# A hand-planned attention block: another account of VectorE's time, other due times, and queries, gating and normalization given out at other places

## The chip, the cores and the metric

The kernel runs on one core of a Trainium2 chip. The metric is the time of one execution on the device in microseconds (us). The kernel before was timed in three runs: 564.36, 565.13 and 567.15, a median of 565.13.

## The reference

The input x has 2 batches of 1024 tokens of 512 channels, all in fp32. Each token is normalized; the result feeds a causal attention with 32 heads of 16 channels, and a gate: a linear layer plus the sum of two of eight low-rank experts (rank 16), chosen for each token. The output is x + s * g.

```python
xn = _layernorm(x)                                   # over the 512 channels
# attention: h = 32 heads, hd = 16
q, k, v = (heads(xn @ W.T + b) for W, b in ((Wq, bq), (Wk, bk), (Wv, bv)))
scores = einsum('bhqd,bhkd->bhqk', q, k) / sqrt(hd)
att = softmax(where(causal, scores, -inf))
s = einsum('bhqk,bhkd->bhqd', att, v).reshape(b, l, d) @ Wo.T + bo
# gate: E = 8 experts of rank R = 16, TOP_K = 2, SCALING = 1
base = xn @ W_base.T + b_base
top_p, top_i = top_k(softmax(xn @ W_gate.T), 2)      # top_p divided by its sum
route_w = sum(one_hot(top_i, E) * top_p[..., None])
delta = einsum('bner,eor->bno', einsum('bnd,erd->bner', xn, A) * route_w[..., None], B)
g = silu(base + delta * SCALING)
out = x + s * g
```

## The kernel before

**Engines and queues.** TensorE (PE) does the products, ScalarE (ACT) the exponentials of the softmax and some copies, VectorE (DVE) evictions, sums and the normalization, GpSimd (POOL) the causal masks, and SyncE (SP) issues nearly all DMAs. Each engine executes its instructions in the order in which the program gives them out. That order is not left to a scheduler: the program is written by a planner in Python that runs once, when the kernel is built.

**The plan.** The attention is cut into units (b, oc, c): a batch, a group of eight heads (128 channels), and a half of 512 queries. A unit with c = 0 has 5 steps, one with c = 1 has 13; a step is a set of key tiles against queries. There are 144 steps. For step n the program gives out, in this order:

- `scores(n)` (from L1513): first what stands in the list `urgent` and is due (placing of keys and queries by DMA), then the score products s <- qT, kT (L1529), then two exponentials pt <- s on ScalarE (L1540);
- the masks of the step on GpSimd (`masked`, L1557: pt <- pt);
- `values(n - 1)` (L1562): the value products av <- pt, v (L1581) with the pt of the step before; at the end of a unit av is copied to oT and avs;
- `fill(n)` (L1426): other work, in small portions, so that TensorE is occupied while ScalarE makes the exponentials.

**Filler work.** `Task` objects are Python generators with a due step, a cost in TensorE's time and conditions. In `fill`, tasks that have a cost give out products until a share is used up; the share is the rest of all work over the rest of the steps, and from step 12 (L1448) it is raised where the work due by some step needs it. After the products, work without a cost on TensorE is given out in this order: entries of `splits`, of `later` (functions with the step from which they may run), tasks without a cost (L1493), then weight blocks (`issue_parts`, L1503), then one or two entries of `late`, which hold evictions of finished product groups.

**The account.** All DVE and ACT instructions go through `Metered` (L40, its call is L56, so L56 is the line of all of them in the profile). It adds up when the engine will be free: 0.09 us plus elements over a rate (930 per us for DVE, 1020 for ACT). `late_by` (L1410) compares DVE's account with the time at which the next step's evictions begin, and `enough(more)` (L1478) says whether `more` us of work would be too late. An entry of `patient` is kept for another step at its first turn if `enough()` is true, and a task without a cost is stopped if its due step is still ahead and `enough(2.0)` (`layernorm_task`) or `enough(0.65)` (others) holds. `SV` = 1.9 stands for the time of scores and values in a step.

**Products by blocks.** The big products (queries and keys "q", values, gate and output "p") are made from 2 x 2 blocks with seven products in place of eight. That needs sums of weight blocks (`four_sums` in `combine_task` and `qk_weights_task`; made once, in place, then stored to DRAM as "kept" and loaded again when needed) and sums of token blocks ("asum", `sums_task`, on DVE). `matmul` (L228) gives out each of the products, 128 x 128 against 256 or 512 columns, as four instructions; it is the line of all filler products. Evictions add the seven products up in kf, qf, v, g and x. Names: ph is the product for routing and experts, pq, pk and pv those of the first unit, made directly.

- `issue_parts` (L613) loads weight blocks ("w" from an input, "wt" from kept, 256 KB each) in the fixed order of their use, up to NWP = 4 ahead of the oldest in use. SP waits at such a load until the buffer's last reader is done.
- `qk_weights_task(n)` (L631) prepares the query and key weights of head group n: for n = 0 to 3 it loads them raw (two DMAs of 256 KB, L123), puts them in pairs with an ACT copy, makes four sums in place on DVE, waits a step, stores them (kept, 1 MB, L640), waits twice more and sets `qk_ready[n]`. For n from 4 (second batch) it loads what was kept. The weights have two buffers. The next load's task waits for `len(qk_ready) >= n` and for the end of the products with the weights of n - 2.
- `split` (L485) turns the finished queries and keys of a unit into qT and kT: DVE and ACT operations, in `later`, then a copy on ACT (`remainder`), then two placing DMAs (L483) put in `urgent` for the next step.
- `layernorm_task(b, c)` (L264): loads x, `statistics` (DVE; then the power -1/2 on GpSimd, L250), subtraction and scaling (DVE), then transposes (sq <- x, DVE), a store to DRAM (scr, L301) and four loads (xnT, L308), in two halves of two channel groups. There is one buffer for sq. For b = 0 the whole second chunk's layernorm falls in the first steps of attention.
- `out_task` (L874): `final` is called with the eviction of an output block; it multiplies by half the gate, adds x, and queues the store, and the load of the next block's x and gate.
- `post` (L1007) normalizes a unit's outputs by the denominators, which go out to DRAM (den, L1020), come back spread (dens, L1025), are inverted, go out (back, L1028) and come back (avs, L1045), whence DVE's rb.

The program ends with a guard that reads a flag and would run a second, general version if scores were out of bounds; here it doesn't run.

Of the kernel before, what the change touches and what calls it, by code (L numbers as in the profile page):

```python
# [13 lines left out]
ALU = mybir.AluOpType  # L14
# [12 lines left out]
KC = D // P  # L27
# [12 lines left out]
class Metered:  # L40


    def __init__(self, engine, rate=930):
        self.engine, self.ready, self.free, self.rate = engine, 0.0, 0.0, rate

    def __getattr__(self, name):
        def run(*args, **named):
            sizes = [1]
            for a in (*args, *named.values()):
                if hasattr(a, "shape"):  # L50
                    n = 1
                    for k in a.shape[1:]:
                        n *= k
                    sizes.append(n)
            self.free = max(self.free, self.ready) + 0.09 + max(sizes) / self.rate
            return getattr(self.engine, name)(*args, **named)  # L56

        return run
# [23 lines left out]
def direct(ctx, tc, sound, x, wq, wk, wv, wo, wb, wa, wg, wB, bq, bk, bv, bo, bb, out):  # L82
# [7 lines left out]


    nc = tc.nc
    ve = Metered(nc.vector)
    act = Metered(nc.scalar, 1020)
    NB, L, _ = x.shape
    C = 512
    NC = L // C
# [119 lines left out]
    WAIT = object()  # L217
    PAUSE = object()
    turned_at, now = {}, [0]
# [44 lines left out]
    def layernorm_task(b, c):  # L264


        xt = chunk_tile(b, c)
        for i in range(NS):
            i0 = c * C + i * P
            nc.sync.dma_start(  # L270
                out=xt[i * SQ : (i + 1) * SQ],
                in_=x[b, i0 : i0 + P].rearrange("(t r) d -> r t d", r=SQ),
            )
        if b == 0:
            load_rest()
        tiles = [xt[:, t] for t in range(TT)]
        for _ in range(3 if b else 1):
            yield WAIT
        s = yield from statistics(tiles, b > 0)
        if b:  # L280
            yield WAIT
        for t in range(0, TT, 2):
            normalize(tiles[t : t + 2], s[0][:, t : t + 2], s[1][:, t : t + 2])
            yield PAUSE
        if b:
            yield WAIT
        xnT = sb.tile([P, KC, C], F32, tag="xnT", bufs=3, name=f"xnT_{b}_{c}")
        for k0 in range(0, KC, 2):
            sq = sb.tile([P, 2, NS, TT, SQ], F32, tag="sq", bufs=1, name="sq")
            for t in range(TT):  # L290
                yield PAUSE
                ve.transpose(
                    out=sq[:, :, :, t],
                    in_=tiles[t][:, k0 * P : (k0 + 2) * P].rearrange(
                        "p (k q d) -> p k q d", k=2, q=NS
                    ),
                )
            scr = dram.tile([NS, SQ, 2, NS, TT * SQ], F32, tag="scr", name="scr")

            def store(sq=sq, scr=scr):  # L300
                nc.sync.dma_start(  # L301
                    out=scr.rearrange("i d k q m -> (i d) (k q m)"),
                    in_=sq.rearrange("p k q t r -> p (k q t r)"),
                )

            def place(k0=k0, scr=scr):
                for q in range(NS):
                    nc.sync.dma_start(  # L308
                        out=xnT[q * SQ : (q + 1) * SQ, k0 : k0 + 2].rearrange(
                            "d k (i m) -> d k i m", i=NS  # L310
                        ),
                        in_=scr[:, :, :, q].rearrange("i d k m -> d k i m"),
                    )

            if not b:
                store()
                place()
                continue
            later.append((now[0] + b, store))
            later.append((now[0] + b + 1, place))  # L320
            for _ in range(0 if k0 else 1 + b):
                yield WAIT
        xnTs[b, c] = xnT
        turned_at[b, c] = now[0] + b
# [160 lines left out]
    def split(b, oc, c, qf, kf):  # L485

        qT, kT = split_tiles(b, oc, c)
        split_keys(kT, kf, kf)

        def queries():  # L490
            split_queries(qT, qf)
            room["acc"] += 1
            later.append((now[0] + 1, remainder))

        def remainder():
            copy_remainder(qT)
            urgent.append((now[0] + 1, lambda: place_queries(qT)))

        by = starts[b, oc, c]
        costs[queries], costs[remainder] = (1.1, by - 4), (0.6, by - 3)  # L500
        later.append((now[0] + 1, queries))
        urgent.append((now[0] + 1, lambda: place_keys(kT, kf)))
# [117 lines left out]
    def qk_weights_task(n):  # L620

        oc = n % KC
        if n >= KC:
            wqks.append(sb.tile([P, 4 * KC, P], F32, tag="wqk", bufs=2, name=f"wqk{oc}"))
            nc.sync.dma_start(out=wqks[n], in_=qk_kept[oc])
        else:
            if n >= 2:
                wqks.append(load_qk(oc))
                for _ in range(3):
                    yield WAIT  # L630
                pair_up(wqks[n])  # L631
                yield WAIT
            w = wqks[n]
            yield from four_sums(
                {(i, j): w[:, 4 * j + 2 * i : 4 * j + 2 * i + 2] for i in range(2) for j in range(2)},
                {t: w[:, 2 * KC + 2 * t - 2 : 2 * KC + 2 * t] for t in range(1, 5)},
            )
            qk_kept[oc] = dram.tile([P, 4 * KC, P], F32, tag=f"kept_qk{oc}", bufs=1, name="kept")
            yield WAIT
            nc.sync.dma_start(out=qk_kept[oc], in_=w)  # L640
            for _ in range(2):
                yield WAIT
        qk_ready[n] = now[0] + (2 if n >= KC else 0)
        yield WAIT

    def tokens(k):
# [227 lines left out]
    def out_task(k):  # L874

        _, b, c = stages[k]
        y, g = block_of(chunk_tile(b, c)), block_of(g_tiles[b, c])
        order = [(0, 0), (1, 1), (0, 1), (1, 0)]
        xts, gts = {}, {}

        def block(t, i, j):
            rows = slice(c * C + BK * i, c * C + BK * i + BK)
            return t[b, rows, BK * j : BK * j + BK].rearrange("(t p) o -> p t o", p=P)

        def load():
            i, j = order[len(xts)]
            xts[i, j] = sb.tile([P, 2, BK], F32, tag="xr", name=f"xr_{b}_{c}_{i}{j}")
            nc.sync.dma_start(out=xts[i, j], in_=block(x, i, j))
            gts[i, j] = sb.tile([P, 2, BK], F32, tag="gr", name=f"gr_{b}_{c}_{i}{j}")
            nc.sync.dma_start(out=gts[i, j], in_=g(i, j))  # L890

        def final(i, j):
            ve.scalar_tensor_tensor(y(i, j), y(i, j), 0.5, gts[i, j], ALU.mult, ALU.mult)
            ve.tensor_tensor(y(i, j), y(i, j), xts[i, j], ALU.add)

            def store():
                nc.sync.dma_start(out=block(out, i, j), in_=y(i, j))

            later.append((now[0] + 2, store))
            if i == j:  # L900
                later.append((now[0] + 2 - i, load))

        load()
        load()
        yield from block_task(k, y, final)
# [395 lines left out]
    for b in range(NB):  # L1301
        for c in range(NC):
# [24 lines left out]
            if not b and not c:  # L1327
# [13 lines left out]
                    )  # L1341
                for n in range(2 * KC):
                    Task(
                        (20, 13, 26, 32)[n] if n < KC else -9, qk_weights_task(n), 0.0, after=9,
                        ready=lambda n=n: n < 2 or (
                            now[0] > qk_done.get(((n - 2) // KC, (n - 2) % KC, 1), now[0])
                            and len(qk_ready) >= n
# [23 lines left out]
                )  # L1371
            else:
                before = starts[b, KC - 1, c] + 2
                Task(len(plan) - 9, bases_task(b, c), 0.0, after=before - 12, takes={"xnT": 2})
                n = len(units) - 3
                Task(len(plan) - 12, test_task(0, n, 0), 0.0, after=before - 10)
                Task(
# [26 lines left out]
    last_work = 13 * MM  # L1404
    spent = 0.0
    late, active = [], []
    SV = 1.9
    clock = [15.0]

    def late_by(n, begins, more):  # L1410
# [4 lines left out]
            return free - begins  # L1415
        if plan[n - 1][3] and plan[n - 1][0] != units[-1]:
            free = max(free, begins + 2.0) + 1.3
        return free - (begins + SV + 1.7 + 0.7)

    def turn_late():  # L1420
        late.sort(key=lambda x: x[0])
# [4 lines left out]
    def fill(n):  # L1426
# [18 lines left out]
        elif n < begin:  # L1445
            even = min(even, (total - last_work - spent) / (begin - n))
        share = spent + even
        if n >= 12:  # L1448

            left = 0.0  # L1450
            for x in tasks:
# [41 lines left out]
        for x in [x for x in tasks if not x.cost]:  # L1493
# [1 line left out]
                continue  # L1495
            said = PAUSE
            while said is not None and said is not WAIT:
                if x.due > n and enough(2.0 if x.steps.__name__ == "layernorm_task" else 0.65):
                    break
                said = x.step()  # L1500
            x.waiting = said is WAIT
        clock[0] = begins
        issue_parts()  # L1503
        for _ in range(1 if active or len(plan) - 5 < n < len(plan) else 2):
            if late and (min(x[0] for x in late) <= n or not within):
# [4 lines left out]
        for par, kt, q0, _, _ in plan[n][1]:  # L1510
            last_pieces.setdefault((par, q0 == C - P), []).append((n, kt, q0))

    def scores(n):  # L1513
        (b, oc, c), pieces, _, _ = plan[n]
        for x in [x for x in urgent if x[0] <= n]:
            urgent.remove(x)
            x[1]()
        ss = [ps_s.tile([P, 2, C], F32, tag="s", name=f"s{p}") for p in range(2)]
        for m, (par, kt, q0, w, col) in enumerate(pieces):
            first_unit = (b, oc, c) == units[0]  # L1520
# [581 lines left out]
```

## Time and profile before

One execution was profiled. It took 567.24 us; its span on the core, first to last instruction, is 565.51.

| what | value |
|---|---|
| median of the three timed runs | 565.13 us |
| the profiled execution, whole | 567.24 us |
| its span | 565.51 us |
| granted TensorE clock, mean | 0.992 of full |
| instructions | 19451 |
| ACT: exponentials pt <- s | 288, 1024 ns each |
| POOL: masks pt <- pt | 224, 512 ns each on average |
| DMA | 79.16 MB, 140 GB/s on average |

How to read the views that follow. The page gives each engine's busy time, its share of the span and the number of instructions; below it the span in 40 equal slices of 14.1 us, a digit being the busy share in tenths (9 is 90% or more), and "PEclk" the granted clock in tenths. In the list of waits, a line names the engine, operation and line that waited, then what released it, then the sum in us, the number of waits and the longest. A line of the timeline has the start, the time until the end, the engine, its line, the operation, written and read tiles, shape, and xcount for the number of like instructions put together; in brackets the engine's idle time just before and what ended it. "SPq" lines are the moments at which SP's queue issued a DMA, not the transfer itself. Busy times are near the limit here: what is left is where TensorE stands still.

### The profile page before, as it was taken

What the parts mean: (1) busy time and instruction counts of PE and PEld (TensorE: products, weight loads), DVE (VectorE), ACT (ScalarE), POOL (GpSimd) and SP (SyncE); (2) the same over time, 40 slices, a digit from 0 to 9 for tenths busy, and PEclk for the clock granted to TensorE, in tenths of its full rate; (3) what the DMA queues carried; (4) which work ended last, traced back from release to release, by engine and by line L of the source; (5) the groups of instructions that cost most, each with busy time, mean ns of one, the idle gap of its engine ahead of it and who ended that gap; (6) DMA issues with size and microseconds to landing.
All of it is one profiled execution on the core that took longest, in us unless ns stands there. A gap on an engine that the chain in (4) does not pass through costs nothing.

```text
span 565.5 us, 19451 instructions
## 1 busy us (share of the span) xinstructions
PE 543.5 (96%) x8411; PEld 283.0 (50%) x8411; DVE 334.5 (59%) x693; ACT 351.8 (62%) x389; POOL 119.0 (21%) x248
## 2 busy tenths in 40 slices
PE   8999998899999999999998999999999999999994
PEld 8434554454445554544644554444545554456551
DVE  4444556557477675566569546684257644649833
ACT  2427852576777766757656765747667777776540
POOL 2213400110114430230213330220103330120400
PEclk9999998999999999999999999999999999999997
DMA  8632576154723663651564633660124223552211
GB/s 254 175 131 78 188 261 208 64 190 134 207 77 139 224 227 118 184 157 60 171 188 152 212 126 114 220 187 23 42 72 157 80 79 90 181 167 82 96 39 45
DMA packets 65198, 79.16 MB, mean 140 GB/s; under 512 B 9560, under 2 KB 52576, under 8 KB 63696
## 3 DMA queue, kind: packets, MB, share of 16 engines
q1 hardware_dynamic: 65088, 77.83, 42.7%
q8 instruction: 68, 1.11, 0.8%
q14 instruction: 26, 0.21, 0.1%
q10 hardware_dynamic: 16, 0.00, 0.0%
HBM read 46.39 MB, written 19.37 MB: 116 GB/s over the span
## 4 chain that ended last, share of the span: by engine, by line
PE 84%; DVE 9%; DMA 2%; ACT 2%; issue 1%; POOL 0%; SPq 0%; DVEq 0%; POOLq 0%; ACTq 0%
PE av L1581 23%; PE p L228 21%; PE s L1529 16%; PE q L228 13%; DVE x L56 3%; PE po L228 2%; PE ph L228 2%; PE pv L228 1%; PE pq L228 1%; PE pk L228 1%; ACT pt L56 1%; PE warm L183 1%; DMA qT<-qT 1%; DVE oT L56 1%; PE pq_first L350 1%
## 5 line engine op out<-in xcount | busy, mean ns | idle before, releaser
L56 ACT ACTIVATE pt<-s 128x1024 f32<-128x1024 f32 x288 | 290.5, 1024 | 166.8 <-PE s L1529 155.7
L1557 POOL TENSOR_SCALAR_AFFINE_SELECT pt<-pt 128x256 f32<-128x256 f32 (+1 forms) x224 | 111.0, 512 | 413.9 <-ACT pt L56 413.0
L1581 PE MATMUL av<-pt,v 128*32 128x512 f32 (+3 forms) x1680 | 158.8, 467 | 3.0 <-DVE oT L56 1.9
L1529 PE MATMUL s<-qT,kT 32*128 32x512 f32 (+3 forms) x1616 | 108.9, 365 | 1.8 <-DMA qT<-qT 1.1
L1529 PEld LDWEIGHTS s<-qT,kT 32*128 32x128 f32 x1616 | 62.4, 184 | 61.2 <-issue 34.4
L1581 PEld LDWEIGHTS av<-pt,v 128*32 128x32 f32 x1680 | 42.6, 109 | 58.5 <-issue 39.7
L228 PE MATMUL p<-wt,asum 128*32 128x256 f32 x960 | 59.8, 383 | 2.2 <-DVE m L56 2.2
L228 PE MATMUL q<-asum,wqk 128*32 128x256 f32 x832 | 51.2, 379 | 3.2 <-DVE kf L56 3.2
L228 PEld LDWEIGHTS p<-wt,asum 128*32 128x32 f32 x960 | 31.8, 111 | 31.1 <-issue 12.1
L228 PEld LDWEIGHTS q<-asum,wqk 128*32 128x32 f32 x832 | 26.5, 110 | 27.9 <-DVE kf L56 6.9
L228 PE MATMUL q<-xnT,wqk 128*32 128x256 f32 x624 | 39.6, 379 | 0.0
L56 DVE TENSOR_TENSOR g<-p,g 128x512 f32<-128x512 f32 x20 | 13.8, 690 | 28.1 <-PE p L228 28.1
L56 DVE SCALAR_TENSOR_TENSOR kf<-q,kf 128x256 f32<-128x256 f32 x39 | 16.5, 422 | 23.5 <-PE q L228 23.1
L228 PEld LDWEIGHTS q<-xnT,wqk 128*32 128x32 f32 x624 | 20.0, 110 | 19.0 <-issue 6.0
L228 PE MATMUL p<-w,xnT 128*32 128x256 f32 x448 | 28.1, 379 | 0.0
L228 PEld LDWEIGHTS p<-w,xnT 128*32 128x32 f32 x448 | 15.8, 110 | 10.6 <-issue 4.2
L228 PE MATMUL p<-w,asum 128*32 128x256 f32 x320 | 20.6, 379 | 0.0
L56 DVE TENSOR_TENSOR v<-p,v 128x512 f32<-128x512 f32 x15 | 10.3, 687 | 12.8 <-PE p L228 12.7
L228 PEld LDWEIGHTS ph<-wag_sb,xnT 128*32 128x32 f32 x512 | 15.4, 110 | 3.8 <-issue 2.7
L228 PE MATMUL ph<-wag_sb,xnT 128*32 128x136 f32 x512 | 16.9, 279 | 0.0
L228 PE MATMUL po<-wo,oT 128*32 128x512 f32 x128 | 16.5, 593 | 0.4 <-ACT oT L56 0.4
L56 DVE TENSOR_TENSOR qT<-qf,qT 128x512 fp32r<-128x512 f32 x15 | 10.3, 686 | 9.9 <-ACT qT L56 9.9
(145 smaller groups left out, 561.4 us busy)
## 6 DMA issues: line engine op xcount, KB each, us to landing
wt<-kept SPq DMA_DIRECT2D x40, 256.0 KB
qT<-qT SPq DMA_DIRECT2D x30, 256.0 KB
x<-in_x_dram SPq DMA_DIRECT2D x16, 256.0 KB
kept<-wqk SPq DMA_DIRECT2D x4, 1024.0 KB
wqk<-kept SPq DMA_DIRECT2D x4, 1024.0 KB
kT<-kf SPq DMA_DIRECT2D x30, 128.0 KB
scr<-sq SPq DMA_DIRECT2D x6, 512.0 KB
xnT<-scr SPq DMA_DIRECT2D x24, 128.0 KB
```

The source lines that it names most:

```text
L56: return getattr(self.engine, name)(*args, **named)
L183: nc.tensor.matmul(warm[:, n % 4 * P : n % 4 * P + P], lhsT=ident, rhs=ident, start=True, stop=True)
L228: nc.tensor.matmul(o[j : j + 32], lhsT=lhsT[:, j : j + 32] if len(lhsT.shape) == 2 else lhsT[:, j // 32], rhs=rhs, start=start, stop=stop,)
L350: nc.tensor.matmul(ps[:, cols], lhsT=w[:, k, :], rhs=xnT[:, k, cols], start=k == 0, stop=k == KC - 1)
L1529: nc.tensor.matmul(ss[s // 2][:, s % 2, col : col + w], lhsT=keys[rows, kt % TT * P : kt % TT * P + P], rhs=q[rows, halves * par + half_, ...
L1557: nc.gpsimd.affine_select(out=d, in_=d, compare_op=ALU.is_ge, fill=0.0, base=0, pattern=[[0, d.shape[1]], [1, P]], channel_multiplier=-1,)
L1581: nc.tensor.matmul(avs_now[par][32 * s : 32 * s + 32, q0 : q0 + w], lhsT=vs[b, kt][:, h * VS - HD * par : h * VS - HD * par + HP], rhs=pt[ ...
```

## The change

Both versions give out the same number of instructions. The change alters when.

1. The account: DVE 0.19 us plus elements / 966 (before 0.09, 930), ACT 0.22 plus elements / 1274 (before 0.09, 1020). `SV` is 1.7 (1.9). A task without a cost stops at `enough(1.85)` if its due step is over 20 steps ahead, else at 0.65; the special value for layernorm goes.
2. Layernorm: the first batch's chunks too wait a step between DVE's statistics and GpSimd's power, and there is a wait for the next step after each half's store and loads.
3. Queries: their placing becomes due in the same step, and `fill` gives out what is urgent just ahead of the weight blocks.
4. Query and key weights: `qk_ready[n]` is set before the step's wait that stands ahead of the store, so up to three steps earlier; the tasks n = 2, 3 are due at 24 and 28 (26, 32).
5. Output blocks: the two gating operations, the store and the next load become one function, in `later` and `patient`, so that evictions can go ahead of it.
6. The rule that raises a step's share for due work holds from step 5 (12). `bases_task` is due 7 steps before the end (9).

```diff
-    def __init__(self, engine, rate=930):
+    def __init__(self, engine, base, rate):
...
-            self.free = max(self.free, self.ready) + 0.09 + max(sizes) / self.rate
+            self.free = max(self.free, self.ready) + self.base + max(sizes) / self.rate
...
-    ve = Metered(nc.vector)
-    act = Metered(nc.scalar, 1020)
+    ve = Metered(nc.vector, 0.19, 966)
+    act = Metered(nc.scalar, 0.22, 1274)
...
-        s = yield from statistics(tiles, b > 0)
+        s = yield from statistics(tiles, True)
...
                 store()
                 place()
+                yield WAIT
                 continue
...
-            urgent.append((now[0] + 1, lambda: place_queries(qT)))
+            urgent.append((now[0], lambda: place_queries(qT)))
...
+            qk_ready[n] = now[0]
             yield WAIT
             nc.sync.dma_start(out=qk_kept[oc], in_=w)
             for _ in range(2):
                 yield WAIT
-        qk_ready[n] = now[0] + (2 if n >= KC else 0)
+        qk_ready.setdefault(n, now[0] + 2)
         yield WAIT
...
         def final(i, j):
-            ve.scalar_tensor_tensor(y(i, j), y(i, j), 0.5, gts[i, j], ALU.mult, ALU.mult)
-            ve.tensor_tensor(y(i, j), y(i, j), xts[i, j], ALU.add)
+            def gated():
+                ve.scalar_tensor_tensor(y(i, j), y(i, j), 0.5, gts[i, j], ALU.mult, ALU.mult)
+                ve.tensor_tensor(y(i, j), y(i, j), xts[i, j], ALU.add)
+                later.append((now[0] + 2, store))
+                if i == j:
+                    later.append((now[0] + 2 - i, load))
...
-            later.append((now[0] + 2, store))
-            if i == j:
-                later.append((now[0] + 2 - i, load))
+            patient.append(gated)
+            later.append((now[0], gated))
...
-                        (20, 13, 26, 32)[n] if n < KC else -9, qk_weights_task(n), 0.0, after=9,
+                        (20, 13, 24, 28)[n] if n < KC else -9, qk_weights_task(n), 0.0, after=9,
...
-                Task(len(plan) - 9, bases_task(b, c), 0.0, after=before - 12, takes={"xnT": 2})
+                Task(len(plan) - 7, bases_task(b, c), 0.0, after=before - 12, takes={"xnT": 2})
...
-    SV = 1.9
+    SV = 1.7
...
-        return free - (begins + SV + 1.7 + 0.7)
+        return free - (begins + SV + 2.4)
...
-        if n >= 12:
+        if n >= 5:
...
-                if x.due > n and enough(2.0 if x.steps.__name__ == "layernorm_task" else 0.65):
+                if x.due > n and enough(1.85 if x.due > n + 20 else 0.65):
...
         clock[0] = begins
+        place_urgent(n)
         issue_parts()
...
+    def place_urgent(n):
         for x in [x for x in urgent if x[0] <= n]:
             urgent.remove(x)
             x[1]()
+
+    def scores(n):
+        (b, oc, c), pieces, _, _ = plan[n]
+        place_urgent(n)
```

More of the change, by code (lines that the diff above doesn't have):

```diff
@@ L40 @@
 class Metered:
-    def __init__(self, engine, rate=930):
-        self.engine, self.ready, self.free, self.rate = engine, 0.0, 0.0, rate
+    def __init__(self, engine, base, rate):
+        self.engine, self.ready, self.free, self.base, self.rate = engine, 0.0, 0.0, base, rate
     def __getattr__(self, name):
@@ L1511, in direct @@
             last_pieces.setdefault((par, q0 == C - P), []).append((n, kt, q0))
-    def scores(n):
-        (b, oc, c), pieces, _, _ = plan[n]
+    def place_urgent(n):
         for x in [x for x in urgent if x[0] <= n]:
```

## The prediction

> **What bounds the kernel now.** First the page: shares of each engine and the 40 slices.
>
> ```profile
> PE 543.5 (96%) x8411; PEld 283.0 (50%) x8411; DVE 334.5 (59%) x693; ACT 351.8 (62%) x389; POOL 119.0 (21%) x248
> PE   8999998899999999999998999999999999999994
> PEclk9999998999999999999999999999999999999997
> ```
>
> TensorE (PE) is busy 543.5 of 565.5 us, so at most 22.0 us can be won without taking work from it; the change takes none (same instructions). VectorE (DVE) and ScalarE (ACT) have a third of the span free: what can matter is only where one of them, or a DMA, is late for TensorE. Slices 1, 7 and 8 and 22 (14 us each) are the thin ones, and in slice 7 the clock too. Next, TensorE's waits:
>
> ```profile
> PE q L228 <- DVE kf L56: 3.2, 3, 1.6
> PE p L228 <- DVE m L56: 2.2, 1, 2.2
> PE av L1581 <- DVE oT L56: 1.9, 2, 1.0
> PE warm L183 <- POOL mhalf L192: 1.4, 1, 1.4
> PE pq L228 <- DVE v L56: 1.2, 1, 1.2
> PE s L1529 <- DMA qT<-qT: 1.1, 1, 1.1
> PE av L1581 <- POOL pt L1557: 0.9, 1, 0.9
> ```
>
> Apart from the start (warm), they are single places, 10.5 us in all. I took each in the timeline. Step 2 has two of them:
>
> ```profile
> 26.15 1.02 POOL L250 TENSOR_TENSOR rstd<-rstd,mhalf 128x4 f32<-128x4 f32 x1 [7.09 <-DVE rstd L56]
> 27.59 1.17 PE L1581 MATMUL av<-pt,v 128*32 128x512 f32 x6 [0.90 <-POOL pt L1557]
> 33.52 1.42 DVE L56 STREAM_TRANSPOSE sq<-x 128x256 f32<-128x256 f32 x4 [2.75 <-DMA scr<-sq]
> 34.87 1.25 DVE L56 TENSOR_TENSOR v<-pv,bv_sb 128x512 f32<-128x512 f32 x2
> 35.58 1.92 PE L228 MATMUL pq<-xnT,wqk 128*32 128x512 f32 x16 [1.24 <-DVE v L56]
> ```
>
> The pow of rstd (26.15) is on POOL ahead of the masks (selects) that the value products need: 0.90. The second four transposes (33.52) wait 2.75 for a buffer that a store reads, and the eviction of v stands behind them: 1.24. Step 4 shows the selects at 3.04 for four, 0.76 each, beside DVE's sums of two SBUF tiles:
>
> ```profile
> 45.47 3.04 POOL L1557 TENSOR_SCALAR_AFFINE_SELECT pt<-pt 128x256 f32<-128x256 f32 x4 [14.85 <-ACT pt L56]
> ```
>
> Step 13 has the longest wait, and the window after it gives the clock (columns: stretch, its length, busy time of PE, PEld, DVE, ACT, POOL, granted clock, DMA share, GB/s):
>
> ```profile
> 83.17 0.50 SPq L616 DMA_DIRECT2D wt<-kept  x1
> 88.22 2.27 PE L228 MATMUL p<-wt,asum 128*32 128x256 f32 x24 [2.22 <-DVE m L56]
> 88.80:92.20 3.40, 3.40 (x32) 1.25 (x25) 0.47 (x3) 0.46 (x1) 0.00 (x0) 0.50 0.72 260
> ```
>
> The page puts the 2.22 down to DVE's m, but no product reads m: the weights wt were issued at 83.17, 5.05 before use, behind two raw loads of wqk. The block came late. After it the clock is halved for 3.40 us, worth 1.70 of work. Last, at 209.63 the scores wait for the queries qT, issued behind a weight block:
>
> ```profile
> 203.96 1.40 SPq L616 DMA_DIRECT2D w<-in_wv_dram  x1
> 205.46 1.19 SPq L483 DMA_DIRECT2D qT<-qT  x2
> 209.63 0.74 PE L1529 MATMUL s<-qT,kT 32*128 32x512 f32 x8 [1.14 <-DMA qT<-qT]
> ```
>
> From the starts of the scores I took the length of every step. An undisturbed one is 3.39 (scores 0.66, values 0.89, 32 product rows 1.84); what a step is longer than its work is its loss, and it is more than the bare waits, for half clock and slow starts are in it. Step 2 loses 2.3; 4: 1.1; 8 to 15: 7.2 together (0.45, 0.92 in 8 and 11, 3.2 in 13, 0.8 in 14, 1.86 in 15); 45: 1.1; 72 and 73: 2.25; 93: 1.15; 129 and 130: 1.8.
>
> [...] the issuing queue itself stands at a wait: SP waits 97.6 us in all for products that free a weight buffer. [...]
>
> **The change part by part**
>
> *Layernorm.* The pow now comes a step's wait later, behind step 1's selects on POOL: the 0.90 goes. The second transposes go to step 3, behind the evictions of v: the 1.24 goes, and with the slow start 2.2 to 2.4 in all. I take −2.3. Next late there is xnT of the second half, wanted only by the products from step 4. In step 4 the selects then run beside transposes (one input) and not sums: between 0 and 1.1 saved, I take −0.7.
>
> *Deadlines from step 5, dues, account.* With the due times applied earlier, steps 5 to 14 get 72 short routing rows, 56 + 8, 24, 32, 32, 32 and four times 40 products, in place of 16 to 48 and then three times 72. So the evictions per step fall, the routing's small DVE operations move to 8 to 12, and the block of step 13 is issued in step 10 and used in 12: some 7 us ahead against 5.05. All five losses of 8 to 15, 7.2 with the 1.70 of clock, have their cause removed: −7.2; the bound on the other side is that only the 2.22 and the clock go, −3.9. The slower account of DVE (0.19 + n/966) holds optional work back more, VectorE being free 41%: nothing by itself. But in step 16 four sums of w_gate (4 × 0.715) and one of 0.42 now stand ahead of an eviction: 3.28 of DVE's work against a step with 2.3 to spare: +0.9 (0 to 1.5).
>
> *qk_ready set before the store.* It lets the third load of query and key weights (wqk2) be given out ahead of the store of wqk0, so it takes the other buffer, wqk1's, whose last reader is a product in step 17. SP's queue is in order: from step 13 to 2.55 after the start of step 17 (call it T17) nothing behind the load is issued. Behind it in the queue stand: a gate weight block, 4 placements of the routing (hwT), a 1 MB store (wqk0), a block, the denominators' way back (back, avs), the 1 MB store of w_gate, two blocks read from it, the next two raw loads, keys, a third 1 MB store (wqk2), then the queries for step 23. Costed with issues of 0.5, 5.05 for a loaded block, 3.9 for a 1 MB store that is read again (59.66 to 63.54 in the timeline) and 2.3 for back to avs (97.87 to 100.16):
> wqk2 lands at T17+5.7. Its pairing copy on ACT (1.17, as at 105.63) stands ahead of step 18's two exps (1.02 each), which end at 8.95, where they would at 5.9: step 20 is 1.6 late. The first block lands at 8.6, wanted at 9.6: just hidden. back and avs land at about 14.3, and DVE's rb operation, waiting for them, holds an eviction that step 22's products need; still 1.6 late. The store of w_gate, issued at 12.7, lands at 16.6; its blocks at 18.8. The queries are issued at 20.3 and land behind 1 MB at about 26.1. Step 23 would begin at T17+21.5 (128.65 − 107.12 before). So 4.7 late there, which includes the earlier 1.6. Low end 2.4 (lands as quickly as the 2.3 of back), high end 6.5 (store and blocks as slow as loaded ones); I take +4.7. A wait over 2.2 can halve the clock once more: 1.7 at a chance of 0.3: +0.5.
>
> *Queries ahead of blocks.* At step 45 qT goes ahead of w: w's issue took 1.40, so 1.14 goes, and I take −1.0; the block behind it has five steps.
> *Gating behind evictions.* In 72 and 73 the two gating operations of a block (0.69 each, as g<-p,g of the same size on the page) stand before evictions and the values' start: 2.25 goes less 0.35, since step 73 then is 2.54 of TensorE's work, and two exps of 1.02 with their waits are what limits: −1.9. Step 93's 1.15 goes also (−1.1). The output's store goes with the gating, at most a step later; the last blocks lie before the tail and there DVE is free. 129, 130 and the last 17 us keep their order: 0. The later base rows: at 138, covered by DVE's free time; if not, 0.3, which I take: +0.3.
>
> *Sum:* −2.3 − 0.7 − 7.2 − 1.0 − 1.9 − 1.1 = −14.2; +0.9 + 4.7 + 0.5 + 0.3 = +6.4. Net −7.8. The profiled execution took 567.24, its span 565.51 and 1.73 around it; so it would come to 559.4. The median of the three timed runs is 565.13, 2.1 below: 557.3, say **557.5**.
>
> **The rivals**
> *A. SP's stop is hidden.* Chance 0.28. If the stores move as fast as in the best window (320 GB/s at 85.00 to 88.30), qT lands in time and pairing is all there is: costs 0.9 + 0.3, net −13.0, 552; with 2.4 at step 23, 554.5. For it: DMA's mean load is 43%. Against: the queue's order leaves no choice to the queries.
> *B. The backlog eats the gain (slower).* Chance 0.06. Behind the stop stand three 1 MB stores and some 2.2 MB of loads ahead of the queries. At the page's mean, 140 GB/s, the 3 MB alone take 22 us and not 10: qT lands 11 later, step 23 is 15.5 late, and two windows at half clock are 3.4: +20.1 − 14.2 = +5.9, 571. It decides from 9.6 late at step 23 (break-even), 12.4 for +0.5%. Against: the queue is then empty of other work, and 260 to 320 GB/s was moved in the busy windows.
> *C. The early losses only move.* Chance 0.14. Fewer rows per step in 8 to 14 pass the same evictions and routing to 5 to 8, which lose as much: 7.2 not gained, net −0.6, 564.5. For it: step 8 already lost 0.45. Against: 13's wait and clock come from one late block.
>
> **How the numbers follow.** Forecast 0.52 (555 to 561), A 0.28 (551 to 555), C 0.14 (561 to 568), B 0.06 (over 568). About 0.5% is what a measurement of this kernel can tell from no change: 562.3 and 568.0. Faster: 0.52 + 0.28 + 0.06 of C = 0.86; same 0.08; slower 0.06. Leaving out some 0.08 below and 0.12 above: 552 to 562.5.
>
> **What would show it.** Right: TensorE's waits for POOL's pt and for v gone; no clock of 0.5 near 85 to 95; SP waiting some 13 us ahead of the load of wqk2; the scores of step 23 waiting for qT by 2 to 3 and the exps of step 18 by about 2 behind a copy; at step 45, 73 and 93 no wait over 0.3. Wrong: waits of 1 or more in steps 5 to 12 (C); scores of step 23 in time (A); half clock in several windows after step 20 (B).

## The result, and the profile after

The changed kernel took 560.80 us (median of nine runs, 559.78 to 563.28); the kernel before 564.62 in as many. The ratio is 0.9935, with a 95% interval of 0.9916 to 0.9954: faster by 0.65%. The forecast was 557.5. The profiled execution took 560.80, its span 559.07, 6.44 less than before; each engine executes as many instructions as before. The counts and TensorE's lines on the page after:

```profile
PE 540.1 (97%) x8411; PEld 279.9 (50%) x8411; DVE 334.4 (60%) x693; ACT 351.5 (63%) x389; POOL 118.6 (21%) x248
PE   8999999789999999999999999999999999999994
PEclk9999999899999999999999999999999999999998
```

Slices 7 and 22 are no longer thin, the first still is; slices 8 and 9 (98 to 126 us) are the thin place now, and in slice 8 the clock is low too. TensorE's waits after say what stands there:

```profile
PE s L1538 <- ACT pt L56: 3.8, 3, 2.8
PE s L1538 <- DMA qT<-qT: 2.3, 1, 2.3
PE q L228 <- DVE qf L56: 1.7, 2, 1.1
```

The longer waits of before (for kf, m, oT, 1.2 us for v, and the masks' pt) are gone; in their place the scores wait for ScalarE (3.8) and for queries (2.3). From the starts of the scores one can draw up a ledger by steps. Every stretch below holds the same product work in both kernels (as many products of each shape), so its difference is waiting and clock alone. The last column puts the terms of the prediction beside the stretches that they speak of.

| steps | before, us | after, us | difference | predicted |
|---|---|---|---|---|
| up to step 0 | 15.14 | 14.92 | -0.22 | 0 |
| 2 to 4 | 25.72 | 21.69 | -4.03 | -3.0 |
| 5 to 16 | 55.85 | 49.13 | -6.72 | -6.3 |
| 17 to 22 | 21.53 | 29.37 | +7.84 | +5.2 |
| 45 | 4.61 | 3.40 | -1.21 | -1.0 |
| 72 to 75 | 16.81 | 14.93 | -1.88 | -1.9 |
| 93 and 94 | 8.00 | 8.25 | +0.25 | -1.1 |
| 138 to the end | 39.86 | 39.40 | -0.46 | +0.3 |
| all others | | | 0.0 | 0 |

The gain is 14.5 and the loss 8.1. The ledger's 6.44 is more than the medians' 3.8, since the profiled execution of the kernel before was a long one: of the 61 executions of it that were timed beside the experiments, the 17 with a mean clock of 0.993 or less have a median of 567.42, the 37 with 0.995 or more one of 565.50, and the profiled one (0.992, 567.24) is like the former. So some 1.7 to 1.9 of what steps 5 to 16 gave is probably half clock that most executions don't have; only one execution of that kernel was profiled, so this is inferred from the mean clocks.

The loss begins on SP's queue, the first two lines of the next view, and is seen in steps 18 and 19:

```profile
98.80 0.38 SPq L123 DMA_DIRECT2D wqk<-in_wq_dram  x1
99.23 0.85 SPq L123 DMA_DIRECT2D wqk<-in_wk_dram  x1
103.94 1.11 ACT L56 COPY wqk<-wqk 128x1024 f32<-128x1024 f32 x1 [3.94 <-DMA hwT<-hscr]
104.95 1.93 ACT L56 ACTIVATE pt<-s 128x1024 f32<-128x1024 f32 x2
106.01 0.50 PE L1538 MATMUL s<-qT,kT 32*128 32x512 f32 x2 [2.83 <-ACT pt L56]
```

Among SP's own waits (the view by queue) one line is new, and it is the longest single wait:

```profile
SPq L123 <- PE q L228: 19.3, 1, 19.3
```

SP stood 19.3 us at the load of wqk2, until the last product that reads the buffer (step 17, which begins at 96.14). The copy that needs this load began at 103.94, 4.7 after the second half's issue. The exps (exponentials) of step 18 stand behind the copy on ScalarE, and the scores of step 19, which need a score buffer that these exps free, begin 2.83 late. In the window from 107.40, just after that, the granted clock is 0.51:

```profile
107.40:110.80 3.40, 3.40 (x42) 1.68 (x40) 0.69 (x1) 2.71 (x3) 0.00 (x0) 0.51 0.18 53
```

At the end of the backlog come the queries for step 23. They were issued at 118.87, behind the 1 MB store of wqk2, and the scores that read them began at 125.51:

```profile
118.30 0.53 SPq L642 DMA_DIRECT2D kept<-wqk  x1
118.87 1.86 SPq L484 DMA_DIRECT2D qT<-qT  x2
```

```profile
125.51 0.74 PE L1538 MATMUL s<-qT,kT 32*128 32x512 f32 x8 [2.34 <-DMA qT<-qT]
```

The other new wait, in step 94, is of the gating that was put off:

```profile
373.08 0.89 DVE L56 SCALAR_TENSOR_TENSOR x<-x,gr 128x512 f32<-128x512 f32 x1 [2.41 <-DMA gr<-kept_g]
376.43 1.93 PE L228 MATMUL q<-asum,wqk 128*32 128x256 f32 x32 [1.09 <-DVE qf L56]
```

DVE stands 2.41 us at the gating, because its gate block's load (gr) was issued only at 368.46, when the gating before it had been given out; two sums and the eviction qf stand behind it.

### The profile page after: what moved, and what is told of

Same layout as the page of the kernel before. It is cut to its first block, busy times and chain, and to the rows that moved or that the text cites. A ratio compares the mean times of both kernels' runs of the same rounds, so it can differ in the third digit from the quotient of the medians.

```text
span 559.1 us, 19432 instructions
## 1 busy us (share of the span) xinstructions
PE 540.1 (97%) x8411; PEld 279.9 (50%) x8411; DVE 334.4 (60%) x693; ACT 351.5 (63%) x389; POOL 118.6 (21%) x248
## 4 chain that ended last, share of the span: by engine, by line
PE 87%; DMA 5%; DVE 3%; SPq 1%; ACT 1%; issue 1%; ACTq 0%; DVEq 0%
PE av L1590 24%; PE p L228 21%; PE s L1538 17%; PE q L228 13%; PE pv L228 2%; PE po L228 2%; PE ph L228 2%; PE pq L228 1%; PE pk L228 1%; DMA qT<-qT 1%; ACT pt L56 1%; DMA back<-rc 1%; DVE x L56 1%; DMA wqk<-in_wq_dram 1%; DMA wqk<-in_wk_dram 1%; DMA gr<-kept_g 1%
## 5 line engine op out<-in xcount | busy, mean ns | idle before, releaser
L228 PEld LDWEIGHTS q<-asum,wqk 128*32 128x32 f32 x832 | 26.5, 110 | 26.1 <-issue 6.9
L56 DVE TENSOR_TENSOR kf<-kf,kT 128x512 f32<-128x512 f32 x15 | 10.3, 684 | 12.1 <-ACT kT L56 12.0
```

The source lines that it names most:

```text
L228: nc.tensor.matmul(o[j : j + 32], lhsT=lhsT[:, j : j + 32] if len(lhsT.shape) == 2 else lhsT[:, j // 32], rhs=rhs, start=start, stop=stop,)
```

## The experiments

The theory: one stop of SP's queue, made by the load of wqk2 passing the store of wqk0, costs all 7.84 of steps 17 to 22; the gains have the parts as causes that the prediction named. The rivals: it is the traffic itself; or the copy on ScalarE is one cost and the queries another; and for the gains, other parts than those named. Times are medians, ratios are against the kernel before in the same comparison, and stretches come from one profile of each kernel. The changed kernel was timed beside the kernel before in the first comparison alone, and from one comparison to the next the median of the kernel before went from 564.62 to 566.38; a difference of medians from two comparisons is no better than that. The stretches are finer: steps 0 and 1 take 10.41 in every profile, and most stretches that an edit leaves alone agree within 0.1; only steps 93 and 94 (by up to 0.6) and the last stretch, from 138 (by up to 0.9), differ more.

**The readiness late again.**

```diff
-            qk_ready[n] = now[0]
             yield WAIT
             nc.sync.dma_start(out=qk_kept[oc], in_=w)
             for _ in range(2):
                 yield WAIT
-        qk_ready.setdefault(n, now[0] + 2)
+        qk_ready[n] = now[0] + (2 if n >= KC else 0)
...
-                        (20, 13, 24, 28)[n] if n < KC else -9, ...
+                        (20, 13, 26, 32)[n] if n < KC else -9, ...
```

> The changed kernel with the fourth part alone undone: qk_ready set again after the store and two waits, due steps 26 and 32. The orders of all engines up to step 12 and of TensorE throughout stay those of the changed kernel; the load of wqk2 stands again behind the store of wqk0. Theory (SP's queue stops at the load from step 13 to 17, and all of what steps 18, 19 and 22 lose comes from it): these three steps give back 2.9 + 2.5 + 2.4 = 7.8 us, so 553.0, SP waits under 3 us ahead of wqk, no half clock after step 16. Rival (it is the traffic of the weights' stores and loads in steps 13 to 23, which must pass at some time): at most the 2.9 of the pairing copy comes back, and the queries of step 23 stay late: 557 to 561.

Measured: 554.14 us, ratio 0.9773 (0.9743 to 0.9804). Steps 17 to 22 take 21.53, as before the change: all 7.84 come back, and no wait for ScalarE or a DMA above 0.5 is left but in the start (`pq_first`):

```profile
PE s L1537 <- ACT pt L56: 1.2, 3, 0.5
PE pq_first L351 <- DMA wqk<-in_wq_dram: 0.9, 1, 0.9
```

Steps 23 to 57 take 122.66 with equal work, against 121.15, because step 31 now gets no filler product, and ScalarE's exps and copies hold up it and step 32 (4.38 in place of 3.39); so the whole is 6.7 better, not 7.8. The rival of mere traffic is out: the same bytes move. The edit undoes the due steps 24 and 28 with the flag, and no run does the one without the other; ready_at_store and rule_12 below keep these due steps and get back 5.4 and 7.0, so the flag and not the due steps is what costs most.

**The pairing copy two steps later, SP's stop kept.**

```diff
-                for _ in range(3):
+                for _ in range(5):
                     yield WAIT
                 pair_up(wqks[n])
```

> The changed kernel with ScalarE's pairing copy of the raw weights two steps later (five waits ahead of it, not three); the load of wqk2 and SP's stop stay. Theory of one stop (everything behind SP's stop is set by the moment at which the queue runs on, so a step that no longer waits only brings the wait for the queries forward to full size): steps 18 and 19 give back 5.4, and step 22 waits longer, 5 to 8 us in place of 2.4; total 558 to 561. Rival (the copy ahead of the exponentials is itself the cost, and the wait for queries a separate one of 2.4): 560.8 - 5.4 = 555.4.

Measured: 559.66, ratio 0.9867 (0.9834 to 0.9899). SP's 19.3 us wait is there as before. Steps 18 and 19 take 3.52 and 3.45 (6.42 and 5.99), so 5.4 come back; but steps 21 and 22 take 9.26 and 4.92 (3.88 and 5.81). TensorE's longest wait is now

```profile
PE p L228 <- DMA wt<-kept: 4.3, 1, 4.3
```

a block read from the stored w_gate, another thing from the same backlog; the clock is 0.50 around its end (6.83 us from 116.58). So of 7.84 only 0.94 is saved. The theory of one stop holds here: what one place gave back the next one lost. That the queries would be what waits was wrong: a block did.

**The due rule from step 12 again.**

```diff
-        if n >= 5:
+        if n >= 12:
```

> The changed kernel with the due rule of shares from step 12 again. Theory (the rule spreads the routing and block products over steps 5 to 14, and that is what gained the 7.5 us of steps 5 to 15): this comes back, less what a later start of step 17 hides of SP's stop; 560.8 + 5 to 7.5 = 566 to 568.5, with the long wait for a weight block and the half clock in step 13 or nearby. Rival (the account and the due steps of weights did it): 560 to 562.

Measured: 555.84, ratio 0.9803 (0.9772 to 0.9834): faster than the changed kernel by 5.0, where I expected slower by 5 or more. Steps 5 to 16 take 51.44: the rule is worth 2.3 of the 6.7 there, not all. And steps 17 to 22 take 22.39: the stop is gone, though qk_ready is set early. SP's queue shows why:

```profile
83.99 0.42 SPq L642 DMA_DIRECT2D kept<-wqk  x1
90.67 0.38 SPq L123 DMA_DIRECT2D wqk<-in_wq_dram  x1
```

Here the store of wqk0 is given out before the load is, so the load gets wqk0's buffer and waits for the store alone. So in the changed kernel it takes both, the rule from step 5 and the early flag, to make the stop. Theory and rival both missed: neither had the stop go.

**The parts alone, on the kernel before.** Layernorm:

```diff
-        s = yield from statistics(tiles, b > 0)
+        s = yield from statistics(tiles, True)
...
                 place()
+                yield WAIT
                 continue
```

> The kernel before with the layernorm part alone (the power a step's wait later for the first batch, and a wait after each half's store). Steps 2 to 4 should give the 4.0 us that they gave in the changed kernel. Theory after rule_12 (the later xnT lets the routing products go ahead of the direct query and key products, so that routing and the load of wqk2 no longer crowd steps 12 to 15): steps 5 to 16 give 4.4 more, in all 8.4 us less than before. Rival (layernorm acts on steps 2 to 4 alone, and the account gave the rest): 4.0 us less, and steps 13 to 15 keep their wait for the weight block and the half clock.

Measured: 560.03, ratio 0.9904 (0.9869 to 0.9939). Steps 2 to 4 take 21.68 (25.72), steps 5 to 16 take 52.48 (55.85), so 4.04 and 3.37, the 7.4 us of the profiles (span 7.6 shorter); by the ratio it is 5.4, for the same reason as above. The theory held with a smaller size (3.4 and not 4.4, and up to 1.7 of it is the half clock after step 13): layernorm acts far beyond the steps that it is in. Step 5 now gets 48 rows of the routing product, where it had 16 of the direct one, so routing goes ahead of the direct queries and keys.

The account:

```diff
...
-    ve = Metered(nc.vector)
-    act = Metered(nc.scalar, 1020)
+    ve = Metered(nc.vector, 0.19, 966)
+    act = Metered(nc.scalar, 0.22, 1274)
```

> The kernel before with the new account alone (0.19 + n/966 for VectorE, 0.22 + n/1274 for ScalarE; SV, thresholds and all else as before). Theory: it moves the load of wqk2 from step 12, ahead of the weight block, to step 15, so the 2.22 us wait of step 13 and the half clock after it go: 3 to 5 us less than before, all in steps 12 to 15. Rival (an account gives out nothing and takes nothing; a planner's better knowledge of VectorE's time is worth nothing where VectorE is free 41%): within 1 us of before.

Measured: 566.30, ratio 1.0007 (0.9994 to 1.002): no difference. Yet steps 5 to 16 take 51.07, 4.8 less, and step 13 has lost its wait for the block as the theory said. Steps from 72 on give another 3.1. But steps 17 to 22 take 2.8 more and 23 to 71 another 3.8, with equal work, in waits like these:

```profile
PE s L1529 <- ACT pt L56: 2.2, 6, 0.5
PE s L1529 <- DMA qT<-qT: 1.8, 1, 1.8
```

The theory was right on steps 12 to 15 and wrong on the total, where the rival's figure holds. (`SV` and the limits 1.85 and 0.65, which belong to the first part too, stayed as before here; no run has them alone.) The rule:

```diff
-        if n >= 12:
+        if n >= 5:
```

> The kernel before with the due rule of shares from step 5, and nothing else. Theory of the prediction (the spread of products over steps 5 to 14 removes their losses by itself): steps 5 to 16 take 6 to 7 us less, TensorE's equal work kept. Rival, from rule_12 (in the changed kernel the rule is worth 2.3 us there, the rest came with other parts): 2 to 3 us less than before.

Measured: 563.40, ratio 0.996 (0.9945 to 0.9975). Steps 5 to 16 take 54.10, 1.75 less; the rival's 2 to 3 is nearer than my 6 to 7. Alone, the rule doesn't take the long wait away: TensorE waits 2.57 ahead of a product p<-wt,asum in step 12 (at 85.58), in place of the 2.22 in step 13, and a half clock stands there (3.41 us from 85.32). Together the three would give 9.9 in steps 5 to 16 if they added; the changed kernel gets 6.7, since layernorm and the account each take away the same wait of step 13 and the clock behind it.

**The readiness set at the store.** One line of the changed kernel is moved:

```diff
-            qk_ready[n] = now[0]
             yield WAIT
             nc.sync.dma_start(out=qk_kept[oc], in_=w)
+            qk_ready[n] = now[0]
```

> The changed kernel with one line moved: qk_ready is set just after the store is given out, not before the step's wait ahead of it; due steps stay 24 and 28. The load of wqk2 then stands in step 15, behind the store of wqk0, and takes that buffer, still two steps earlier than in late_ready. Theory (the stop came from the load passing the store, and so from the buffer it got, not from being early): SP stands at the load for 3 us at most, steps 17 to 22 take 21.5, total 553 to 554.5 as in late_ready. Rival (an early load of the weights crowds the queue in steps 13 to 22 in any case): steps 17 to 22 keep 3 us or more of their loss, 556.5 or more.

Measured: 555.70, ratio 0.9831 (0.9792 to 0.9869). Steps 17 to 22 take 24.01: 5.4 of 7.84 are gone, 2.5 stay. SP waits 6.8 at the load, from the store (83.09) to 90.30, more than the 3 I allowed:

```profile
83.09 0.38 SPq L641 DMA_DIRECT2D kept<-wqk  x1
90.30 0.39 SPq L123 DMA_DIRECT2D wqk<-in_wq_dram  x1
```

What stays is 0.9 in step 20, where the pairing copy again stands ahead of two exps, and 1.6 in step 22, before the queries of step 23, which stand behind the store of wqk2 and the loads of wqk3:

```profile
104.26 1.19 ACT L56 COPY wqk<-wqk 128x1024 f32<-128x1024 f32 x1
120.03 0.73 PE L1538 MATMUL s<-qT,kT 32*128 32x512 f32 x8 [1.55 <-DMA qT<-qT]
```

So two thirds of the loss came from which buffer the load got. The third that stays goes with weights that come early, as the rival said; how much of it is SP's remaining stop of 6.8 us, this run can't tell. Neither expectation was met whole.

**Gating two steps after its load's issue**, on late_ready and on the kernel just shown:

```diff
+            loaded[i, j] = now[0]
             gts[i, j] = sb.tile([P, 2, BK], F32, tag="gr", ...)
...
-            later.append((now[0], gated))
+            later.append((max(now[0], loaded.get((i, j), now[0]) + 2), gated))
```

> As late_ready, and the gating of an output block is put two steps or more after the issue of its gate's load, so that VectorE doesn't stand at it with an eviction behind. Theory (step 94's 1.36 us are VectorE's wait for the load of gr): 1.3 less than late_ready, 551.7. Rival (VectorE simply has too much to do in steps 92 to 95, and the gating must be done there): the loss moves by a step, same as late_ready within 0.5.

> As ready_at_store, and the gating of an output block two steps or more after the issue of its gate's load. Theory: steps 93 and 94 take 6.84 as in late_ready_gate, 0.8 to 1.4 less than ready_at_store. Rival: the gain of late_ready_gate was chance between two profiles; same within 0.3.

Measured: 552.84 (0.975, 0.9719 to 0.9781) against 554.14, and 553.64 (0.9792, 0.9757 to 0.9828) against 555.70. Steps 93 and 94 together take 6.85 in both (7.68 and 8.20), steps 72 to 75 0.4 less. The wait for gr was the cause, and the rival, chance between two profiles, is out: the same step lost the same wait twice, 0.8 of the 1.3 expected on late_ready and 1.35 on the other. 552.84 is the fastest version that I ran.

**The sums of w_gate later**, on late_ready_gate:

```diff
-                if x.due > n and enough(1.85 if x.due > n + 20 else 0.65):
+                if x.due > n and enough(1.85 if x.due > n + 20 or x.steps.__name__ == "combine_task" else 0.65):
```

> As late_ready_gate, and the sums of w_gate's blocks are given out only where 1.85 us of VectorE's time are free (0.65 before), so that they no longer stand ahead of an eviction in step 16. Theory (0.8 us of step 16 is an eviction behind these sums, as the prediction had it): step 16 takes 4.3, not 5.06, and 0.7 us less in all, 552.1. Rival (the sums come later, so their store and the blocks read from it, wanted at about step 21, come too late): a wait for wt of 1 to 4 us in steps 20 to 22, total 553 to 556.

The edit holds for every `combine_task`; at step 16 that is the one of w_gate. Measured: 558.11, ratio 0.9884 (0.9846 to 0.9921), 5.3 worse (4.6 by the spans). Step 16 takes 4.26 in place of 5.06, so the prediction's 0.9 is shown to be those sums (0.8); but steps 17 to 22 take 28.04 (21.53). It is the rival's mechanism: the wait has the size that it named, and with the half clock after it (3.41 us) the total goes beyond its 553 to 556:

```profile
PE p L228 <- DMA wt<-kept: 3.9, 1, 3.9
```

**Gating with the eviction again, and queries behind blocks again**, each on late_ready:

```diff
         def final(i, j):
-            def gated():
-                ve.scalar_tensor_tensor(...)
...
+            ve.scalar_tensor_tensor(...)
+            ve.tensor_tensor(...)
```

> As late_ready, but with the gating, its store and load given out with the eviction again (the fifth part undone). Theory (the gating stood ahead of evictions in 73 and 93): steps 72 to 75 take 16.8, not 14.93, and steps 93 and 94 take 8.0, not 7.7: 2.2 us more than late_ready, 556.3. Rival (once the account holds VectorE's optional work back, these evictions are on time in either order): same as late_ready within 0.5.

Measured: 554.64 (0.9798, 0.9754 to 0.9842). Steps 72 to 75 take 14.92: no change. Steps 93 and 94 take 7.34, 0.3 less, which is within their scatter. Only the last stretch, from 138, takes 1.15 more: in step 140 DVE's sums of the last outputs and the final test stand before the copy avs, and TensorE's transposes (the second line) wait for it; the step takes 4.53 and not 3.56.

```profile
522.46 1.01 DVE L56 COPY avs<-av 128x384 f32<-128x384 f32 x2
523.06 0.89 PE L228 MATMUL pt_o<-ident,avs 128*32 128x128 f32 x16 [0.52 <-DVE avs L56]
```

The rival was right for steps 72 to 75: the gating stands ahead of the copy oT there as it did before the change, and TensorE doesn't wait. The account is a part of the cause. The runs with 14.93 have only 16 product rows in step 73 and 48 in 74, and so has account_alone; the kernel before and the other two parts alone have 32 and 32, and take 16.81. But account_alone takes 16.21, so the new rates give 0.6 of the 1.88 by themselves (in step 74 a product waits 0.94 for a sum of tokens, asum). Which part gives the other 1.3 isn't shown.

```diff
-            urgent.append((now[0], lambda: place_queries(qT)))
+            urgent.append((now[0] + 1, lambda: place_queries(qT)))
...
         clock[0] = begins
-        place_urgent(n)
         issue_parts()
```

> As late_ready, but queries are placed a step later and behind the weight blocks again (the third part undone). Theory (the 1.2 us of step 45 are the block's issue ahead of qT): step 45 takes 4.6, not 3.40, the other units' queries are early enough: 1.2 more, 555.3. Rival (with the other parts the transfers have moved, and the queries are in time anyway): same as late_ready within 0.4.

Measured: 554.52 (0.9801, 0.9757 to 0.9845). Step 45 takes 3.40 in both. But in late_ready and this run these queries are placed in step 43, not 44, so the run can't show what their place does in the changed kernel itself. There the trace has qT ahead of the block, at 200.78 in step 44, and no wait; that this is the cause remains argued. A rival stands: account_alone leaves the queries' placing as it was, and there too they are issued in step 44 (203.25), ahead of the block, and step 45 takes 3.40. So the gain can come without the third part.

## Why the prediction was right or wrong

The direction, the range and the mechanism of the loss were right; the time was 3.3 too low, and several gains were put down to the wrong part. The gain was forecast at twice its size: by the medians it is 3.8 us, and the prediction took off 7.6. Of the 3.3, 1.4 is in the sum (−7.8 against −6.44, so 559.4 against the profiled 560.80). The other 1.9 is the last step, "the median of the three timed runs is 565.13, 2.1 below": the profiled execution before held the half clock of step 13, which most executions lack by their mean clocks. So the 1.70 was counted as a gain for the profile and was not one for the median; taking off 2.1 once more was wrong, as the after profile lies at its median.

Some of the agreement is luck. Steps 5 to 16 came to −6.72 against −6.3 though the split behind the figure was wrong, and the loss, 2.6 larger than forecast, was made up in part by layernorm (1.0 more) and by the last stretch (0.8 more).

- *Layernorm* (−3.0): −4.03. Step 4 gave 1.10, the upper end of "between 0 and 1.1", not 0.7: its four selects took 1.68 beside the transposes (at 42.31), where they had taken 3.04 beside the sums; that the other operation on DVE makes this difference was an estimate of mine, and no run has it alone. Step 2 gave 2.94 where 2.3 was taken; its two bare waits are 2.14 of that, and what the other 0.8 is isn't shown. What the step left out is that the same edit reorders steps 5 to 16 (norm_alone: 3.4 there).
- *Deadlines, dues, account* (−7.2, and +0.9 for w_gate's sums): −6.72, near the −6.3. The sum was near, its split wrong: the rule that the prediction described is worth 1.75 alone and 2.3 in the changed kernel. The rows that it foresaw (72 short routing rows in step 5 and so on) did come in the changed kernel, but not from the rule by itself: alone it gives step 5 24 rows of the direct product, and routing comes first only with the layernorm part (48 rows in step 5 of norm_alone). "The slower account ... nothing by itself" was right for the whole time and wrong as a statement about steps 5 to 16, where it gives 4.8. The +0.9 was right (0.8, shown by late_gate_sums).
- *qk_ready before the store* (+4.7, +0.5 for clock): +7.84. The chain was right link by link: load into wqk1's buffer, SP's stop to 2.66 after the start of step 17, copy ahead of exps, queries last. It took the rule from step 5 as well, though, which the prediction didn't say (rule_12). SP waited 19.3 us ahead of the load, from step 13 to step 17 as the chain had it; the 13 us that the prediction gave as a sign did not fit its own chain. Mis-sized were three terms. wqk2's pairing began 7.8 after step 17's start, not 5.7, as the second load took 4.7 from issue to use. The delay came a step sooner, since the scores of step 19 wait for a score buffer that the exps free: 2.9 in step 18, not 1.6. And the half clock, put in at 0.5, came by the mean clocks in all nine executions (0.993 or less, where those of late_ready have 0.994 or more): of the 2.5 lost in step 19, up to 1.7 is this (3.40 us at 0.51). "A wait over 2.2" was an estimate from the one wait of step 13; the 2.34 us in step 23 had no half clock after it. The queries came at 29.4, not 26.1.
- *Queries ahead* (−1.0): −1.21 in step 45, place right, cause not isolated: it can come from the account too. *Gating* (−1.9): −1.88 in steps 72 to 75, a figure met by luck, as late_gate_first shows that the gating's place does not give it; the account's other spread of products gives 0.6, and the rest stays open. *Step 93* (−1.1): its 1.16 went and 1.41 came in step 94. The prediction asked what is late next for the store and not for the load, which had gone behind the gating too: a load that follows a deferred operation, and the next operation that waits for it.
- *The later base rows* (+0.3): the last stretch is 0.46 shorter, which is within its scatter, and no run has the base rows alone. The gating's part gives 1.15 there on late_ready, which the prediction had at nothing, on the ground that DVE is free there; in step 140 it isn't.
- *The rivals.* A (the stop is hidden) is out: steps 17 to 22 lost 7.8. It named 552 for that case; late_ready, which has all but the stop, comes to 554.1. B's backlog was real but broke off at 7.8 late, below its 9.6. C is refuted by the ledger: steps 5 to 16 take 6.7 less for equal work.

## What to carry to other kernels

A flag that lets a load be given out earlier also decides which buffer the load gets: look for the last reader of that buffer and count everything behind the load on its issuing queue. A forecast made per place in the timeline can be right while its causes are wrong; where a planner sets the order, only each part alone, and all but each, tell whose gain it is, and parts that remove the same wait don't add. Moving work behind evictions moves its loads as well.

## What the runs showed of the hardware

TensorE's clock. Every profile has half clock (0.50) in its last 3.5 to 6.3 us, when the products are over: 5.7 us before the change, 4.5 after it. Between the start and that, five of the fourteen have it once more, for 3.41 us (6.83 in copy_later), and in each it begins within 1.7 us of the end of the longest wait that TensorE has: 2.22 us (before), 2.57 (rule_5_alone), 2.83 (after), 3.91 (late_gate_sums), 4.31 (copy_later). The nine profiles whose longest wait is 1.84 or less have none; their mean clocks are 0.994 to 0.997, those of the five 0.990 to 0.993. The mean clocks of all timed executions agree: 0.993 or less in all 19 of the three kernels with a wait of 2.83 or more, in 17 of 61 of the kernel before, in 4 of 20 of rule_5_alone, and in none of the other 62. That the wait brings the half clock is read from this order; no run changes the wait alone, and where between these waits it sets in isn't shown: the 2.34 us in step 23 of the changed kernel's profile had none after it (1.00 from 123.00 to 133.00). A stretch of 3.41 us at 0.50 takes up to 1.7 us of work.

In ready_at_store SP stood 6.8 us at the load of wqk2, behind the 1 MB store that reads the same buffer (the store was issued at 83.09, the load at 90.30; the DMA engines moved 348 GB/s from 83.00 to 86.00, 170 from there to 90.30), and 6.2 in rule_12. The prediction had counted 3.9 from a store's issue to the issue of the load that reads it back.
